# Spreading softmax reciprocals: two small transposes and eight SBUF transfers in place of four whole transposes

## The chip, the cores and the metric

The kernel runs on one core of one Trainium2 chip. The metric is the device time of one execution in microseconds (us); lower is better. A core has a tensor engine (PE, with PEld for its weight loads), a vector engine (DVE), a scalar engine (ACT), GpSimd (POOL) and a sync engine (SP), which here only issues transfers. Each works through its own instructions in order.

## The reference, cut to what matters

A decoder layer over 32 sequences of 256 tokens with 256 features: self attention with rotary positions and ALiBi, windowed cross attention, and a feed-forward block with quantized activations, each followed by a residual and a layer norm. The change is in the self attention alone:

```python
# per sequence: x [256, 256]; 16 heads of 64; 4 key/value heads
q, k = rope(x @ Wq), rope(x @ Wk)           # v = x @ Wv
attn = q @ k.T / sqrt(64) + slope[h] * (j - i)
attn = softmax(attn)                        # over the 256 keys j
out = concat_heads(attn @ v) @ Wo
x = layernorm(x + out)
```

The softmax's division by the row sums is done after the product with v: `attn @ v` is formed from the plain exponentials, and each head's output is multiplied by the reciprocal of its sums.

## The kernel before

The work of a sequence is cut into units. A self unit is 128 queries, one of two halves of the key/value heads and two of four head pairs; there are eight per sequence (`self_units`). One step of the outer loop works on the self unit of that step, and a pair of units (`m`, four per sequence) shares one set of sums, one attention output `oT` and one set of reciprocals. A step has two parts (`part` 0 and 1). The order of PE, DVE and ACT is written out by hand in this loop; the order on SP and POOL is chosen by the framework's planner.

In step 2m+2 (an even one), for pair `m`:

- `self_inverse` (L436, L438) runs first: DVE takes the reciprocal of eight columns of sums (128 queries x 8 heads) and copies it out to `wide`, 128 x 512, each column repeated 64 times.
- The generators of the other stages that are due run next: projections (L334 on PE, L343 and L350 on DVE, whose halves are exchanged by the transfers of L316), the query and key rotation of the cross attention (L553 on ACT, transfers of L558, L569 to L571 on POOL), the normed outputs, the feed-forward block (L808 to L859).
- `self_turn` transposes the exponentials `p` of the last unit on PE (L450), and ACT copies them out of PSUM (L455).
- `self_scores` makes the scores of this step's unit (L397); DVE adds the bias and finds the maximum (L413), ACT takes the exponential and sums it (L423).
- `self_values` multiplies the transposed exponentials by v (L467); ACT copies the result to `oT` (L474), where a partition is one of two heads x 64 features and a column is one of 4 x 128 queries.
- In part 1, `self_spread` (L482) transposes `wide` in four products, so that PSUM holds each reciprocal along the partitions of its head, and `self_normal` (L490) multiplies `oT` by that on DVE.

`self_output` later multiplies `oT` by Wo in two halves, in two parts of a later step (L498). Cross-attention steps (L659 scores, L673 maximum, L689 exponential, L698 transposes, L714 values, L734 and L740 back-transposes and division) run interleaved with these. `work(name, shape, bufs)` gives a buffer in SBUF, `bank(name)` one of eight in PSUM. Transfers issued as `nc.sync.dma_start` go through SP's queue.

Of the kernel before, what the change touches and what calls it, by code (L numbers as in the profile page):

```python
# [10 lines left out]
BF16 = mybir.dt.bfloat16  # L11
# [5 lines left out]
P = 128  # L17
# [8 lines left out]
H, KV, HD = 16, 4, 64  # L26
# [24 lines left out]
def kernel(  # L51
# [27 lines left out]
    nc = tc.nc  # L79
    B = x.shape[0]  # L80
# [4 lines left out]
    def ctile(shape, dtype, name):  # L85
        return const.tile(shape, dtype, name=name, tag=name)
# [3 lines left out]
    def bank(name, shape=(P, 512), dtype=F32):  # L90
        return ps.tile(list(shape), dtype, tag="b", name=name)


    ident = ctile([P, P], F32, "ident")
    make_identity(nc, ident)
    ident_b = ctile([P, P], BF16, "ident_b")
    make_identity(nc, ident_b)
    neg_half = ctile([P, 2], F32, "neg_half")
    nc.gpsimd.memset(neg_half, -0.5)

# [3 lines left out]
    def work(name, shape, bufs=2, dtype=F32):  # L104
        return sb.tile(list(shape), dtype, tag=name, name=name, bufs=bufs)

    def small(name, n):
        return sb.tile([P, 8], F32, tag="small", name=name, bufs=48)[:, 0:n]
# [87 lines left out]
    def flush():  # L196
        while last:
            last.pop(0)()
# [190 lines left out]
    def self_scores(b, i):  # L389
        s = state[b]  # L390
        qc, kc, rp = self_units[i]
        qT, kT = s["qT", 2 * kc + rp], s["kT"]
        banks = [bank("s") for _ in range(2)]
        for rr in range(2):
            for half in range(2):
                rows_ = slice(half * HD, (half + 1) * HD)
                nc.tensor.matmul(  # L397
                    banks[half][:, rr * L : (rr + 1) * L],
                    qT[rows_, rr, qc * P : (qc + 1) * P],
                    kT[rows_, kc, :],  # L400
                    start=(rr == 0),
                    stop=(rr == 1),
                )
        s["p", i] = [work("p", [P, 512], 4) for _ in range(2)]
        if rp == 0:
            s["sums", i // 2] = small("sums", 8)
        for half in range(2):
            p = s["p", i][half]
            nm = small("nm", 2)
            for rr in range(2):  # L410
                cols = slice(rr * L, (rr + 1) * L)

                nc.vector.tensor_tensor_reduce(  # L413
                    p[:, cols],
                    banks[half][:, cols],
                    alibi[:, 2 * (4 * kc + 2 * rp + rr) + half, :],
                    -0.125,
                    3.0e38,
                    ALU.add,
                    ALU.min,  # L420
                    nm[:, rr : rr + 1],
                )
                nc.scalar.activation(  # L423
                    p[:, cols],
                    p[:, cols],
                    AF.Exp,
                    bias=nm[:, rr : rr + 1],
                    scale=-1.0,
                    accum_out=s["sums", i // 2][:, (2 * rp + rr) * 2 + half : (2 * rp + rr) * 2 + half + 1],
                )  # L430

    def self_inverse(b, m):

        s = state[b]
        rinv = small("rinv", 8)
        nc.vector.reciprocal(rinv, s.pop(("sums", m)))  # L436
        s["rinv", m] = wide = work("wide", [P, 8, HD], 1)
        nc.vector.tensor_copy(wide, rinv.unsqueeze(2).to_broadcast([P, 8, HD]))  # L438

    def self_turn(b, i):  # L440
        s = state[b]
# [34 lines left out]
    def self_spread(b, m):  # L476

        s = state[b]
        wide = s.pop(("rinv", m))
        s["R", m] = pr = bank("R")  # L480
        for r in range(NCH // 2):
            nc.tensor.transpose(  # L482
                pr[:, r * P : (r + 1) * P], wide[:, 2 * r : 2 * r + 2, :].rearrange("p a e -> p (a e)"), ident
            )

    def self_normal(b, m):
        s = state[b]
        qc, kc, _rp = self_units[2 * m]
        oT = s["oT", qc, kc].rearrange("p c t -> p (c t)")
        nc.vector.tensor_tensor(oT, oT, s.pop(("R", m)), ALU.mult)  # L490
# [400 lines left out]
    with tc.manual_schedule(engines={mybir.EngineType.PE, mybir.EngineType.DVE, mybir.EngineType.Activation}):  # L891
        running = []
        slot = min(starts)
        while starts or running:
            step, part = divmod(slot, 2)
            k, odd = divmod(step - CROSS, 2)
            for gen in starts.pop(slot, ()):
                running.append([slot, gen])

            def cross(f, unit, *more):  # L900
                if 0 <= unit < 4 * B:
                    f(*divmod(unit, 4), *more)

            def own(f, unit):
                if 0 <= unit < 8 * B:
                    f(*divmod(unit, 8))


            def pair(f):
                if step % 2 == 0 and 0 <= step // 2 - 1 < 4 * B:  # L910
                    f(*divmod(step // 2 - 1, 4))

            if part == 0:
                pair(self_inverse)
            else:
                pair(self_spread)
            if part == 1 and not odd:
                cross(cross_exp, k, 0)
            if part == 0 and odd:
                cross(cross_exp, k, 1)  # L920
            for r in list(running):
                if r[0] == slot:
                    wait = next(r[1], r)
                    if wait is r:
                        running.remove(r)
                    else:
                        r[0] += wait or 1
            if part == 0:
                own(self_turn, step - 1)
                if odd:  # L930
                    cross(cross_back, k - 1)
                    cross(cross_turn, k, 0)
                else:
                    cross(cross_turn, k - 1, 1)
                while late:
                    late.pop(0)()
                flush()
                own(self_scores, step)
                if not odd:
                    cross(cross_scores, k)  # L940
                pair(self_values)
            else:
                if not odd:
                    cross(cross_values, k - 1)
                pair(self_normal)
                while late:
                    late.pop(0)()
            flush()
            slot += 1
# [89 lines left out]
```

## Time and profile before

| | |
|---|---|
| Time, median of 3 runs | 2258.0 us (2257.89 to 2258.37) |
| The profiled execution | 2257.97 us, span 2256.0 us |
| Mean granted clock of PE | 0.984 |
| PE busy | 2188.3 us, 97% of the span |
| DVE busy | 1708.6 us, 76% |
| ACT busy | 1680.8 us, 75% |
| POOL busy | 1126.7 us, 50% |
| DMA, queue 1 (SP's and the like) | 189440 packets, 136.95 MB, 24.8% of 16 engines |

The span is from the first to the last instruction of the profiled execution; its time is the device time of the same execution. Busy shares are means over all stages. PE's products are pipelined, so what a group of them costs is the distance from its start to the start of the next group. A row of a timeline has the start in us, the duration, the engine and line, the operation and the names of what is written and read; "x8" counts instructions that were merged into the row.

### The profile page before, as it was taken

The numbers are of one execution on the slowest core, as the hardware profiler recorded it, in microseconds if no ns is written. First come the engines' busy times: TensorE is split into PE (matmuls) and PEld (weight loads), VectorE is DVE, ScalarE is ACT, GpSimd is POOL, SyncE is SP. The second block draws the span as 40 slices with busy tenths as digits, with TensorE's granted clock in tenths as the row PEclk, the third lists the DMA queues.
The fourth block names the chain that finished last, engine by engine and source line by source line (L and its number), as shares of the span: only waits on it lengthen the run. The fifth ranks groups of instructions, "written<-read, shape, count | busy, mean of one in ns | idle before, by whom it ended". The sixth has DMA issues, their size and how long they took to land.

```text
span 2256.0 us, 55618 instructions
## 1 busy us (share of the span) xinstructions
PE 2188.3 (97%) x17828; PEld 1660.7 (74%) x17828; DVE 1708.6 (76%) x6949; ACT 1680.8 (75%) x4961; POOL 1126.7 (50%) x1851
## 2 busy tenths in 40 slices
PE   7999999999999999999999999999999999999983
PEld 5777777777777777777777777777777777777652
DVE  3777777877777877777877778787777887777765
ACT  2677777878777878777878777878777878777862
POOL 5345455555555555555555555555555454545432
PEclk8999999999999999999999999999999999999986
DMA  6322232222222222222222222222222222222111
GB/s 217 90 54 56 63 69 61 55 62 60 64 70 59 59 58 60 68 65 60 60 59 65 63 65 61 62 59 65 60 65 64 61 58 69 56 61 56 34 32 31
DMA packets 191426, 144.07 MB, mean 64 GB/s; under 512 B 107808, under 2 KB 160928, under 8 KB 191136
## 3 DMA queue, kind: packets, MB, share of 16 engines
q1 hardware_dynamic: 189440, 136.95, 24.8%
q8 instruction: 143, 2.34, 0.4%
q10 hardware_dynamic: 1696, 3.57, 0.4%
q14 instruction: 147, 1.20, 0.2%
HBM read 39.50 MB, written 8.39 MB: 21 GB/s over the span
## 4 chain that ended last, share of the span: by engine, by line
PE 89%; DVE 4%; ACT 3%; DMA 2%; POOL 1%; issue 1%; SPq 0%; POOLq 0%; ACTq 0%; DVEq 0%
PE proj L334 13%; PE s L397 11%; PE o L467 10%; PE wo L498 10%; PE t L450 9%; PE xt L698 5%; PE ff L808 4%; PE xs L659 3%; PE R L482 3%; PE xo L714 3%; PE xv L619 3%; PE ffo L855 2%; PE xq L535 2%; PE xw L766 2%; PE xk L607 2%; PE v L366 2%
## 5 line engine op out<-in xcount | busy, mean ns | idle before, releaser
L423 ACT ACTIVATE p<-p,nm 128x256 f32<-128x256 f32 x1024 | 508.7, 501 | 104.8 <-DVE nm L413 100.7
L413 DVE CUSTOM_DVE_ANT_0 p<-s,alibi 128x256 f32<-128x256 f32 x1024 | 372.5, 420 | 124.7 <-PE s L397 124.5
L455 ACT COPY pT<-t 128x512 f32<-128x512 f32 x512 | 273.8, 589 | 224.8 <-PE t L450 224.7
L689 ACT ACTIVATE xp<-xp,xnm 128x128 f32<-128x128 f32 x1024 | 325.8, 393 | 1.8 <-DVE xnm L673 1.8
L397 PE MATMUL s<-kT,qT 64*128 64x256 f32 x2048 | 290.4, 402 | 0.0
L450 PE MATMUL t<-ident,p 128*128 128x128 f32 x2048 | 275.2, 274 | 3.8 <-ACT p L423 2.5
L450 PEld LDWEIGHTS t<-ident,p 128*128 128x128 f32 x2048 | 238.9, 141 | 45.4 <-ACT qb L553 8.4
L467 PE MATMUL o<-pT,v 128*64 128x256 f32 x2048 | 257.0, 386 | 0.2 <-ACT pT L455 0.2
L334 PE MATMUL proj<-xT,wq_sb 128*128 128x256 f32 x1024 | 252.2, 390 | 0.0
L498 PE MATMUL wo<-wo_sb,oT 128*128 128x256 f32 x1024 | 245.3, 382 | 0.0
L358 POOL TENSOR_TENSOR qT<-qT,other 128x512 f32<-128x512 f32 x128 | 163.4, 1277 | 155.0 <-DMA other<-psin 89.8
L673 DVE CUSTOM_DVE_ANT_0 xp<-xs,mask 128x128 f32<-128x128 f32 x1024 | 225.8, 286 | 0.0
L397 PEld LDWEIGHTS s<-kT,qT 64*128 64x128 f32 x2048 | 176.2, 186 | 59.2 <-issue 41.3
L498 PEld LDWEIGHTS wo<-wo_sb,oT 128*128 128x128 f32 x1024 | 192.0, 190 | 35.5 <-issue 10.3
L467 PEld LDWEIGHTS o<-pT,v 128*64 128x64 f32 x2048 | 142.2, 136 | 99.0 <-issue 32.0
L334 PEld LDWEIGHTS proj<-xT,wq_sb 128*128 128x128 f32 x1024 | 187.8, 193 | 33.6 <-DVE xnm L673 6.0
L423 ACT ACTIVATION_READ_ACCUMULATOR p<-p,nm 128x1 f32 x1024 | 195.6, 191 | 0.0
L343 DVE TENSOR_TENSOR psin<-proj,rs_sb 128x512 f32<-128x512 f32 x160 | 110.2, 689 | 93.6 <-PE proj L334 93.3
L569 POOL TENSOR_TENSOR qb<-qb,rx_sb 128x256 f32<-128x256 f32 (+1 forms) x96 | 87.5, 911 | 184.6 <-DMA other<-qb 77.8
L700 ACT COPY xpT<-xt 128x512 f32<-128x512 f32 x256 | 153.6, 600 | 6.3 <-PE xt L698 5.5
L698 PE MATMUL xt<-ident,xp 128*128 128x128 f32 x1024 | 155.1, 274 | 0.0
L823 DVE SCALAR_TENSOR_TENSOR gu<-gu,ff 128x512 f32<-128x512 f32 x128 | 82.3, 682 | 74.6 <-ACT gu L822 74.5
(150 smaller groups left out, 4373.5 us busy)
## 6 DMA issues: line engine op xcount, KB each, us to landing
other<-psin SPq DMA_DIRECT2D x640, 64.0 KB, 2.0
xT<-in_xt_dram SPq DMA_DIRECT2D x32, 256.0 KB, 2.9
xs<-in_x_dram SPq DMA_DIRECT2D x32, 256.0 KB, 3.0
cs<-in_ctx_dram SPq DMA_DIRECT2D x32, 256.0 KB, 2.7
other<-qb SPq DMA_DIRECT2D x64, 128.0 KB, 2.0
kTz<-tr SPq DMA_DIRECT2D x256, 32.0 KB, 2.0
other<-qb SPq DMA_DIRECT2D x128, 64.0 KB, 1.9
out_dram<-x SPq DMA_DIRECT2D x32, 256.0 KB, 2.3
```

Of the source, the lines that this page charges most:

```text
L334: nc.tensor.matmul(pq[:, c * L : (c + 1) * L], w[:, dc, c * P : (c + 1) * P], xT[:, dc, :], start=(dc == 0), stop=(dc == NDC - 1),)
L358: nc.gpsimd.tensor_tensor(d2, d2, other, ALU.add)
L397: nc.tensor.matmul(banks[half][:, rr * L : (rr + 1) * L], qT[rows_, rr, qc * P : (qc + 1) * P], kT[rows_, kc, :], start=(rr == 0), stop=(r ...
L413: nc.vector.tensor_tensor_reduce(p[:, cols], banks[half][:, cols], alibi[:, 2 * (4 * kc + 2 * rp + rr) + half, :], -0.125, 3.0e38, ALU.add ...
L423: nc.scalar.activation(p[:, cols], p[:, cols], AF.Exp, bias=nm[:, rr : rr + 1], scale=-1.0, accum_out=s["sums", i // 2][:, (2 * rp + rr) * ...
L450: nc.tensor.transpose(pt[:, j * P : (j + 1) * P], p[half][:, rr * L + kk * P : rr * L + (kk + 1) * P], ident,)
L455: nc.scalar.copy(pT[half], pt)
L467: nc.tensor.matmul(po[half * HD : (half + 1) * HD, rp * L : (rp + 1) * L], s["v"][:, kk, (2 * kc + half) * HD : (2 * kc + half + 1) * HD], ...
L498: nc.tensor.matmul(py[:, 0:D], s["oT", qc, kc][:, r, :], wo_sb[:, 4 * kc + r, :], start=(kc == 0 and r == 0), stop=(kc == 1 and r == 3),)
L673: nc.vector.tensor_tensor_reduce(p[:, cols], banks[2 * half + j // 2][:, j % 2 * P : (j % 2 + 1) * P], s["mask"][:, qc, :], -1.0, 3.0e38, ...
L689: nc.scalar.activation(p[:, cols], p[:, cols], AF.Exp, bias=s["xnm", i][half][:, j : j + 1], scale=-1.0)
L698: nc.tensor.transpose(pt[:, j * P : (j + 1) * P], p[:, j * P : (j + 1) * P], ident)
```

## The change

The columns of the sums are put in another order (first the four of half 0, then the four of half 1). The reciprocals stay a 128 x 8 tile; `wide` and its copy go. `self_spread` now transposes four columns at a time, in two products that each fill 4 x 128 of a PSUM bank. DVE copies these 4 x 256 values to `rT` in SBUF. Eight transfers on SP's queue then write `R` (128 x 512 in SBUF): each reads one row of 128 values of `rT` and writes it to 64 partitions. `self_normal` multiplies `oT` by `R` from SBUF.

The calls move too: `self_spread` from part 1 to part 0 of the same step, behind `self_turn`; `self_normal` from part 1 of step 2m+2 to part 0 of step 2m+3, behind that step's `self_turn`. An identity in bf16 that nothing uses goes.

```diff
-    ident_b = ctile([P, P], BF16, "ident_b")
-    make_identity(nc, ident_b)
...
-                    accum_out=s["sums", i // 2][:, (2 * rp + rr) * 2 + half : (2 * rp + rr) * 2 + half + 1],
+                    accum_out=s["sums", i // 2][:, half * 4 + 2 * rp + rr : half * 4 + 2 * rp + rr + 1],
...
     def self_inverse(b, m):
-        rinv = small("rinv", 8)
+        s["rinv", m] = rinv = small("rinv", 8)
         nc.vector.reciprocal(rinv, s.pop(("sums", m)))
-        s["rinv", m] = wide = work("wide", [P, 8, HD], 1)
-        nc.vector.tensor_copy(wide, rinv.unsqueeze(2).to_broadcast([P, 8, HD]))
...
     def self_spread(b, m):
-        wide = s.pop(("rinv", m))
-        s["R", m] = pr = bank("R")
+        rinv = s.pop(("rinv", m))
+        pr = bank("R")
+        for half in range(2):
+            nc.tensor.transpose(pr[0:4, half * P : (half + 1) * P], rinv[:, half * 4 : half * 4 + 4], ident)
+        rT = work("rT", [4, 2 * P], 1)
+        nc.vector.tensor_copy(rT, pr[0:4, 0 : 2 * P])
+        s["R", m] = R = work("R", [P, 512], 1)
         for r in range(NCH // 2):
-            nc.tensor.transpose(
-                pr[:, r * P : (r + 1) * P], wide[:, 2 * r : 2 * r + 2, :].rearrange("p a e -> p (a e)"), ident
-            )
+            for half in range(2):
+                nc.sync.dma_start(
+                    R[half * HD : (half + 1) * HD, r * P : (r + 1) * P],
+                    rT[r : r + 1, half * P : (half + 1) * P].unsqueeze(1).to_broadcast([1, HD, P]),
+                )
...
             if part == 0:
                 pair(self_inverse)
-            else:
-                pair(self_spread)
...
             if part == 0:
                 own(self_turn, step - 1)
+                pair(self_spread)
+                if step % 2 and 0 <= step // 2 - 1 < 4 * B:
+                    self_normal(*divmod(step // 2 - 1, 4))
...
             else:
                 if not odd:
                     cross(cross_values, k - 1)
-                pair(self_normal)
```

## The prediction

> **What bounds the kernel now.** I read the page's busy shares and its chain of waits, then the groups of instructions by line, then the timelines of PE, SP, DVE and ACT around the middle of the run.
>
> The chain that ended last says where a saving counts:
>
> ```profile
> PE 89%; DVE 4%; ACT 3%; DMA 2%; POOL 1%; issue 1%; SPq 0%; POOLq 0%; ACTq 0%; DVEq 0%
> ```
>
> PE carries 89% of it, line 482 (the four transposes) about 3%. The PE timeline over one of the short stretches (start, duration, line; a group's end overlaps the next group, so what a group costs is the distance between starts):
>
> ```profile
> 1209.33 1.04 PE L450 MATMUL t<-ident,p 128*128 128x128 f32 x8
> 1210.20 0.38 PE L734 MATMUL xr<-ident,xoT 128*128 128x128 f32 x2
> ...
> 1213.90 0.66 PE L482 MATMUL R<-ident,wide 128*128 128x128 f32 x4
> 1214.39 1.03 PE L808 MATMUL ff<-ff_gate,xiT 128*128 128x512 bf16 x4
> ...
> 1223.02 1.30 PE L450 MATMUL t<-ident,p 128*128 128x128 f32 x8
> ```
>
> Eight transposes take 0.87 us (1209.33 to 1210.20), 0.109 each; the four of line 482 take 0.49, 0.05 of it the semaphore instruction that goes ahead of them in 93 of 128 cases. A sequence repeats every 67.35 us (line 334 starts at 1140.14, 1207.50, 1274.85) with hardly a gap on PE, 32 times. It holds four pairs of steps, counted from the transposes of an even step: A from 1209.33 (13.7 us), B from 1223.02 (15.45), C from 1238.47 (17.3), D from 1255.77 (20.9). Each pair makes one R and multiplies one oT.
>
> The SP queue, where the new transfers go, in pair A and into B:
>
> ```profile
> 1210.78 2.45 SPq L316 DMA_DIRECT2D other<-psin  x4
> 1219.60 5.27 SPq L643 DMA_DIRECT2D kTz<-tr  x8
> 1225.29 1.18 SPq L558 DMA_DIRECT2D other<-qb  x2
> ```
>
> One issue holds SP for 0.6 us, whatever its size (2.45 for 4, 1.18 for 2). From issue to landing:
>
> ```profile
> other<-psin SPq DMA_DIRECT2D x640, 64.0 KB, 2.0
> kTz<-tr SPq DMA_DIRECT2D x256, 32.0 KB, 2.0
> ```
>
> And what is thin on ACT at the end of pair A:
>
> ```profile
> 1219.85 0.51 ACT L423 ACTIVATE p<-p,nm 128x256 f32<-128x256 f32 x1
> ...
> 1221.84 1.27 ACT L689 ACTIVATE xp<-xp,xnm 128x128 f32<-128x128 f32 x4
> 1223.01 0.60 ACT L553 ACTIVATE qb<-xq,xbcol 128x128 f32<-128x128 f32 x2
> ```
>
> ACT runs without a break from the first self exponential to line 553, and the second half of PE's transposes at 1223.02 already waits 0.29 us for line 553 (it reads the bank that they need). So in pair A anything that delays the first line 413 on DVE delays PE by the same time. In the other pairs there is slack.
>
> [...] All eight transfers read rows 0 to 3 of rT. The trace of before has no transfer that reads one partition. [...]
>
> **The change part by part.** Removed on PE: four transposes, 0.49 us a pair. Added: two, 0.22 (0.27 with a semaphore). Gain 0.22 to 0.27 a pair, I take 0.27: 128 x 0.27 = 35 us if nothing waits. This is on the path.
>
> DVE: the copy to wide goes (128 x 0.485 = 62 us), a copy of 4 x 256 from PSUM comes (nearest rows: 0.42 for 256 columns from PSUM, 54 us at most). DVE is not the bound; nothing follows from the sum. The identity in bf16 costs POOL two instructions of 0.5 us before 1.8 us, when PE waits for weights until 4.55: nothing, and with that cover gone 0.5 us once. The column order of the sums costs nothing.
>
> New position of the transposes: right after those of p. They wait for the reciprocal. In C it ends at 1238.65 and PE gets there at 1239.34; in B at 1223.80 against 1224.19. Hidden by the eight transposes; without that cover a few tenths in a pair.
>
> The eight transfers: SP issue 8 x 0.6 = 4.9 us a pair, 128 x 4.9 = 630 us. SP has it (about 1,300 issues of 0.6 us and 128 transposing ones of 1.25 us or more, some 1,000 of 2256 us), but in order: behind them wait psin, qb and kTz transfers, and R waits behind those that come first. I take R behind the transfers whose data is ready first. The landing of the last is bounded by: below, the issue spacing, 2.0 + 7 x 0.61 = 6.3 us from the first issue; above, [...]10.3 us. I take the upper[...] and keep the lower for the range.
>
> The multiplication (0.67) moves to the next odd step, after the transposes and ahead of line 413. DVE, in order, then waits for R, and behind it stand line 413, so the exponentials, so PE's next transposes; and in B and D line 498's second half needs oT. Pair by pair, upper price:
> - A: psin's transfers hold SP until 1213.23. R has landed at 1213.23 + 10.3 = 1223.5, the multiplication ends at 1224.2, the first exponential starts 0.52 later at 1224.75 instead of 1219.85. Line 553 and PE's transposes move with it: +4.9 us.
> - B: transposes end at 1224.4 plus latency, copy until about 1225.0, R landed 1235.3, oT at 1236.0. Line 498 wants it at 1234.13, less 0.27 saved: 2.1 us of waiting, against before +2.0 with a handoff.
> - C: psin's first four hold SP until 1242.2; R landed 1252.5, exponentials from 1253.7 instead of 1252.07, line 553 done at 1257.4 where PE wants the bank at about 1256.2: +1.3, less 0.27: +1.0.
> - D: psin's until 1260.2, R landed 1270.5, line 413 stood at about 1270.1, next transposes only at 1276.68: hidden, -0.27.
>
> Sum 4.9 + 2.0 + 1.0 - 0.3 = 7.6 us per sequence, x 32 = 244: span 2256 + 244 = 2500. The profiled execution took 2257.97, 1.97 more than its span and within 0.03 of the median 2258.0; so 2502.
>
> With the lower price: A has R at 1219.5, exponentials at 1220.7, +0.9. B has R at 1232.8, before DVE comes free at 1233.8: -0.2. C -0.1, D -0.3. Sum +0.3 us, 2268. So the fate of this change hangs on pair A and on when R lands.
>
> **Rivals.** First, [...]the planner's order on SP is kind (R ahead of part of psin's transfers, or psin's ready sooner): all R are hidden, and what stays is PE's gain of 0.27 less a few tenths in A, where the multiplication now stands between line 823 and line 413: 10 to 35 us, 2223 to 2248. For it: SP is idle from 1213.2 to 1219.6 and the engines of the DMA are 25% busy. Second, the lower price as worked out above, 2255 to 2300: only A waits[...]. Third, worse than forecast: R is issued behind a waiting transfer (SP waits 281 us for psin in all, up to 7.7 at a time), or R's packets hold up the qb and psin transfers behind them and PE waits for qT or xqT: 2580 and more. The sign turns at about 0.6 us per transfer, where R in A lands before 1219. That the products do not get fewer is excluded, since two are issued for four.
>
> **How the numbers follow.** [...] 0.58, time 2502, own range 2340 (0.9 us per transfer: A +2.9, the rest about -0.5) to 2620. Lower price: 0.15. Everything hidden: 0.22. SP's order ruinous: 0.05. A measurement can tell about 0.2%, 4.5 us, from no change. Faster 0.25 (the hidden case and a little of the lower price), same 0.05, slower 0.70. The range of 2240 to 2580 leaves out about 0.1 on each side.
>
> **What would show it.** Line 482's successor: 256 products of one group of two, 0.22 us from start to start. R's transfers: 1024 of 32 KB, median landing well over 2 us (4 to 6)[...]. Idle of DVE ahead of line 490 put down to the DMA of R: some 8 us per sequence at the upper price, under 1 at the lower. PE idle for ACT at line 450 and for DVE at line 498; busy share of PE under 90%. I am wrong if DVE's idle before line 490 stays small, or if R lands in 2 us and PE waits all the same.

## The result and the profile after

The changed kernel takes 2929.67 us (2922.08 to 2940.11, 4 runs) against 2258.18 us for the kernel before, run beside it: 1.2978 times as long, 95% interval 1.2962 to 1.2993. "Slower" was forecast, but with 2502 us, and 2580 at the upper end. The loss is 671 us where 244 were forecast.

The profiled execution has a span of 2927.9 us. Lines have moved in the new file: 482 is now 478 (the products) with 484 (the transfers), 490 is 493, 316 is 314, 397 is 395, 413 is 411, 423 is 421, 436 is 434, 450 is 446, 498 is 501, 535 is 538, 553 is 556, 643 is 646, 659 is 662, 714 is 717, 808 is 811. In the experiments they shift by a few more.

The chain that ended last, by engine, on the page of the kernel after:

```profile
PE 34%; DMA 20%; SPq 19%; DVE 13%; POOL 6%; issue 5%; ACT 3%; DVEq 0%; POOLq 0%; ACTq 0%
```

PE carried 89% before. Now 39% is transfers and their issue: the kernel is no longer bound by PE, which is busy 82% of the span. The multiplication on the same page, with DVE's idle time ahead of it behind the second bar:

```profile
L493 DVE TENSOR_TENSOR oT<-oT,R 128x512 f32<-128x512 f32 x128 | 88.6, 692 | 596.7 <-DMA kTz<-tr 204.3
```

The transfers, from issue to landing (all data written) in the last column:

```profile
R<-rT SPq DMA_DIRECT2D x1024, 32.0 KB, 5.2
...
cs<-in_ctx_dram SPq DMA_DIRECT2D x32, 256.0 KB, 6.2
...
kTz<-tr SPq DMA_DIRECT2D x256, 32.0 KB, 2.3
```

and one line of the page before:

```profile
cs<-in_ctx_dram SPq DMA_DIRECT2D x32, 256.0 KB, 2.7
```

R's 32 KB take 5.2 us to land, kTz's 32 KB take 2.3. Others land later too: the load of cs went from 2.7 us to 6.2.

Pair A in the SP timeline of the kernel after (the prediction shows the same stretch without R):

```profile
1404.21 2.49 SPq L804 DMA_TRANSPOSE xiT<-xib  x2
1406.80 0.53 SPq L110 DMA_DIRECT2D xT<-in_xt_dram  x1
1407.43 2.47 SPq L314 DMA_DIRECT2D other<-psin  x4
1410.00 6.50 SPq L484 DMA_DIRECT2D R<-rT  x8
1416.61 6.66 SPq L646 DMA_DIRECT2D kTz<-tr  x8
```

Eight issues of R hold SP for 6.50 us: the first five take up to 0.60 us each, the last three 0.87, 1.15 and 1.26. That the queue pushes back on the issuer is a reading of this; no run isolates it. In the trace these eight transfers land from 1413.22 to 1421.56: the first 3.2 us after its issue, the others one after another, 1.19 us apart in the mean. And the same pair on DVE, on ACT and on PE:

```profile
1421.94 0.69 DVE L493 TENSOR_TENSOR oT<-oT,R 128x512 f32<-128x512 f32 x1 [6.47 <-DMA kTz<-tr]
1422.55 0.42 DVE L411 CUSTOM_DVE_ANT_0 p<-s,alibi 128x256 f32<-128x256 f32 x1
```

```profile
1423.07 0.51 ACT L421 ACTIVATE p<-p,nm 128x256 f32<-128x256 f32 x1 [6.69 <-DVE nm L411]
```

```profile
1403.95 1.04 PE L446 MATMUL t<-ident,p 128*128 128x128 f32 x8
...
1416.05 1.04 PE L811 MATMUL ff<-ff_up,xiT 128*128 128x512 bf16 x4
1423.38 2.08 PE L538 MATMUL xq<-zT,xq_w 128*128 128x128 f32 x8 [6.29 <-DVE nm L411]
...
1426.82 1.89 PE L811 MATMUL ff<-ff_up,xiT 128*128 128x512 bf16 x4
1428.50 1.26 PE L446 MATMUL t<-ident,p 128*128 128x128 f32 x8
```

DVE stands idle 6.47 us ahead of the multiplication. The bracket names a kTz transfer, but line 493 reads nothing of kTz: it waits for R's eight transfers, the last of which, issued at 1415.24, lands at 1421.56. The name is only that of a transfer in the queue near it. Behind the multiplication stands line 411.

PE then stops for 6.29 us at line 538, put down to line 411. No input of line 538 comes from line 411; what they share is a PSUM bank. `bank` hands out eight in turn: counted from the scores ahead of the stop, two go to these scores, four to the cross scores (line 662) and two to the feed-forward products (line 811), so line 538 gets the first bank of the scores again, and may write there only when line 411 has read it. The times agree: the second of the two instructions of line 411 that read this bank ends at 1423.31, and PE goes on at 1423.38.

When PE goes on, the same work takes longer: line 811 took 1.04 us at 1416 and takes 1.89 at 1426. The share of the clock granted to PE shows why. The trace has it in pieces of 3.41 us; here the pieces around this stop, and two around a shorter one in pair C (stretch, its length, PE busy with its instructions, granted clock, DMA share, GB/s):

```profile
1415.31:1418.72 3.41, 1.78 (x18) 1.00 0.71 26
1418.72:1422.13 3.41, 0.00 (x0) 1.00 0.64 61
1422.13:1425.54 3.41, 2.16 (x10) 0.50 0.18 41
1425.54:1428.96 3.42, 3.42 (x41) 0.50 0.11 38
1428.96:1432.37 3.41, 3.41 (x31) 1.00 0.12 7
...
1463.10:1466.51 3.41, 1.36 (x22) 1.00 0.30 83
1466.51:1469.92 3.41, 3.41 (x9) 0.50 0.01 5
```

After the stop PE runs at half its clock, until 1428.96. In pair C the half clock, 0.50 from 1466.51, follows a stop of only 2.00 us:

```profile
1465.62 0.64 PE L717 MATMUL xo<-xpT,xvaug 128*32 128x128 f32 x16 [2.00 <-DVE nm L411]
1466.31 3.62 PE L332 MATMUL proj<-xT,wq_sb 128*128 128x256 f32 x8
```

The same eight products of line 332 took 1.99 us at 1402.12.

### The profile page after: what moved, and what is told of

Same layout as the page of the kernel before. It is cut to its first block, busy times and chain, and to the rows that moved or that the text cites. A ratio compares the mean times of both kernels' runs of the same rounds, so it can differ in the third digit from the quotient of the medians.

```text
span 2927.9 us, 56259 instructions
## 1 busy us (share of the span) xinstructions
PE 2392.1 (82%) x17572; PEld 1744.4 (60%) x17572; DVE 1703.7 (58%) x6949; ACT 1694.8 (58%) x4961; POOL 1108.4 (38%) x1849
## 4 chain that ended last, share of the span: by engine, by line
PE 34%; DMA 20%; SPq 19%; DVE 13%; POOL 6%; issue 5%; ACT 3%; DVEq 0%; POOLq 0%; ACTq 0%
SPq L484 13%; DMA R<-rT 7%; PE proj L332 6%; DMA other<-psin 6%; PE wo L501 5%; DVE p L411 4%; DMA kTz<-tr 3%; SPq L314 3%; PE o L463 3%; DVE oT L493 3%; PE t L446 2%; PE s L395 2%; PE xo L717 2%; PE xq L538 2%; SPq L646 2%
## 5 line engine op out<-in xcount | busy, mean ns | idle before, releaser
L493 DVE TENSOR_TENSOR oT<-oT,R 128x512 f32<-128x512 f32 x128 | 88.6, 692 | 596.7 <-DMA kTz<-tr 204.3
L501 PE MATMUL wo<-wo_sb,oT 128*128 128x256 f32 x1024 | 303.5, 449 | 153.7 <-DVE oT L493 153.6
L501 PEld LDWEIGHTS wo<-wo_sb,oT 128*128 128x128 f32 x1024 | 223.6, 225 | 213.7 <-DVE oT L493 177.4
L446 PE MATMUL t<-ident,p 128*128 128x128 f32 x2048 | 282.1, 281 | 16.6 <-ACT p L421 16.3
L446 PEld LDWEIGHTS t<-ident,p 128*128 128x128 f32 x2048 | 250.5, 146 | 61.7 <-ACT p L421 24.0
L332 PE MATMUL proj<-xT,wq_sb 128*128 128x256 f32 x1024 | 266.7, 407 | 1.3
L538 PE MATMUL xq<-zT,xq_w 128*128 128x128 f32 x512 | 101.1, 358 | 185.4 <-DVE nm L411 185.4
L332 PEld LDWEIGHTS proj<-xT,wq_sb 128*128 128x128 f32 x1024 | 196.3, 201 | 40.4 <-DVE nm L411 8.8
L538 PEld LDWEIGHTS xq<-zT,xq_w 128*128 128x128 f32 x512 | 85.9, 254 | 210.9 <-DVE nm L411 200.2
L600 POOL TENSOR_SCALAR mask<-ck,cq_sb 64x128 f32<-64x128 f32 (+1 forms) x96 | 70.6, 736 | 311.8 <-DVE xnm L676 305.8
```

The costliest lines, as they stand in the source:

```text
L332: nc.tensor.matmul(pq[:, c * L : (c + 1) * L], w[:, dc, c * P : (c + 1) * P], xT[:, dc, :], start=(dc == 0), stop=(dc == NDC - 1),)
L446: nc.tensor.transpose(pt[:, j * P : (j + 1) * P], p[half][:, rr * L + kk * P : rr * L + (kk + 1) * P], ident,)
L501: nc.tensor.matmul(py[:, 0:D], s["oT", qc, kc][:, r, :], wo_sb[:, 4 * kc + r, :], start=(kc == 0 and r == 0), stop=(kc == 1 and r == 3),)
L538: nc.tensor.matmul(pq[:, ch * P : (ch + 1) * P], xq_w[:, dc, ch * P : (ch + 1) * P], zqT[:, dc, :], start=(dc == 0), stop=(dc == NDC - 1),)
```

## The experiments

All times are medians, each beside the kernel before, run with it (2256.9 to 2258.7 us). In the cuts, `...` stands for lines left out. The first set asked what makes R late. Theory 1 in the expectations is that reading from the same few partitions, here 0 to 3, sets the pace: in the kernel after R's transfers land 1.24 us apart in the median.

**Rows four partitions apart.** As after, with the eight rows in partitions 0, 4, ... 28:

```diff
-        nc.vector.reciprocal(rinv, s.pop(("sums", m)))
+        r8 = small("rinv", 8)
+        nc.vector.reciprocal(r8, s.pop(("sums", m)))
+        s["rinv", m] = rinv = work("rinv32", [P, 32], 2)
+        nc.vector.tensor_copy(rinv.rearrange("p (a e) -> p a e", e=4), r8.unsqueeze(2).to_broadcast([P, 8, 4]))
...
-            nc.tensor.transpose(pr[0:4, half * P : (half + 1) * P], rinv[:, half * 4 : half * 4 + 4], ident)
...
+        nc.tensor.transpose(pr[0:32, 0:P], rinv, ident)
...
-                    rT[r : r + 1, half * P : (half + 1) * P].unsqueeze(1).to_broadcast([1, HD, P]),
+                    rT[4 * (4 * half + r) : 4 * (4 * half + r) + 1, :].unsqueeze(1).to_broadcast([1, HD, P]),
```

> The eight reciprocal rows are copied out [...](rows 0, 4, ... 28; one product of 32 columns in place of two of four, and one more small copy on DVE). Everything else as after. Theory 1 ([...]1.2 us or more each, so R lands late): median landing of R falls from 5.2 us to 2.0-2.6, issues take 0.6 us again, the time falls to 2240-2330. Theory 2 (the price is that of eight issues and eight landings on SP's queue, whatever they read): landing stays at 4-5 us, the time stays above 2800.

2401.29 us, ratio 1.063 (1.0611 to 1.0648). The landing fell to 2.8 us, a little over what theory 1 said; the time did not fall as far as it said. So moving the rows apart takes away 528 of the 671 us, and 143 have another cause.

**Rows in partitions 0 to 7.** One product of the eight columns as they are:

```diff
-            nc.tensor.transpose(pr[0:4, half * P : (half + 1) * P], rinv[:, half * 4 : half * 4 + 4], ident)
...
+        nc.tensor.transpose(pr[0:8, 0:P], rinv, ident)
...
-                    rT[r : r + 1, half * P : (half + 1) * P].unsqueeze(1).to_broadcast([1, HD, P]),
+                    rT[1 * (4 * half + r) : 1 * (4 * half + r) + 1, :].unsqueeze(1).to_broadcast([1, HD, P]),
```

> As after, but one product of all eight columns, so the eight rows lie in partitions 0 to 7[...]. Theory 1: [...]landing about 2.7-3.5 us, time 2350-2650[...]. Theory 2: landing 4-5 us, above 2800.

2403.63 us, ratio 1.0637 (1.0621 to 1.0653), landing 2.8 us: no different from rows four partitions apart. In both, R's transfers land 0.63 to 0.64 us apart (median), close to the 0.61 us that one issue holds SP; in the kernel after they land 1.24 us apart. Rows in partitions 0 to 7 are spread enough, and what is left is the spacing of the issues.

**Rows 32 or 64 partitions on.** To tell whether it is how many partitions are read that counts, or which, two kernels that differ in one number, the partition at which half 1's rows begin (`off` is 32 or 64; the columns in between hold ones):

```diff
+        nc.tensor.transpose(pr[0 : 2 * off, 0:P], rinv_wide, ident)
...
+                    rT[half * off + r : half * off + r + 1, :].unsqueeze(1).to_broadcast([1, HD, P]),
```

> The rows of half 0 lie in partitions 0 to 3 and those of half 1 in partitions 32 to 35: eight partitions, each read by one transfer[...]. One product of 64 columns makes them; the rest as after. [...]as after, 2850-2950 us, median landing about 5 us. Rival (what hurts after is that a partition is read by two transfers, or that they are few partitions): as with rows 0 to 7, 2390-2420, landing 2.8 us.

> The same kernel as the run before it, with half 1 in partitions 64 to 67 in place of 32 to 35[...]. [...]2385-2420 us, landing 2.8 us. Rival: no difference to the run before it.

2924.7 us with 32 (ratio 1.2957, 1.2938 to 1.2976) and 2401.39 us with 64 (1.0638, 1.0622 to 1.0654). From the lists of transfers, first with 32, then with 64:

```profile
R<-rT SPq DMA_DIRECT2D x1024, 32.0 KB, 5.2
```

```profile
R<-rT SPq DMA_DIRECT2D x1024, 32.0 KB, 2.8
```

Eight partitions, each read once, are as slow as four read twice when the second half begins at partition 32, and 523 us faster when it begins at 64. So it is neither the number of partitions nor that each is read twice: what counts in these runs is which partitions the rows lie in.

**No transfers.** The products and places of after, with a constant in place of R, so that the division is left out:

```diff
-        s["R", m] = R = work("R", [P, 512], 1)
-        for r in range(NCH // 2):
...
+        s["R", m] = R_const
```

> As after, with the eight transfers left out: line 493 multiplies by a constant tile of ones in place of R (so the division by the sums is left out). Shows what the rest of the change is worth. Theory 1 and 2 both: 2223-2250, the gain of two products a pair with everything hidden. Theory 3 (the new places of the products and of the multiplication make PE wait by themselves): above 2300.

2277.51 us, ratio 1.0084 (1.0069 to 1.0099). Neither expectation held: without a single transfer the change still costs 19 us. Who PE waited for most in this kernel (total us, times, longest):

```profile
PE wo L497 <- DVE oT L489: 19.4, 30, 1.6
```

Line 497 is the output product. In B it comes to DVE's multiplication before DVE has got there.

**The old place.** The same, with the multiplication back in part 1 of the even step:

```diff
-                if step % 2 and 0 <= step // 2 - 1 < 4 * B:
-                    self_normal(*divmod(step // 2 - 1, 4))
...
                     cross(cross_values, k - 1)
+                pair(self_normal)
```

> As the run without transfers (line 493's multiplier is a constant, the division by the sums is left out), with the multiplication back in part 1 of the even step, where it stood before. Separates the new place from the two products less. If the place is what cost the run without transfers its gain: 2220-2235. If the two products less are worth nothing: 2255-2280.

2250.86 us, ratio 0.997 (0.996 to 0.998): faster than before, by 7 us and not by the 28 to 35 that the products alone were to be worth. So the new place of the multiplication costs about 27 us, and three quarters or more of the products' gain is missing. Part of what is missing is shown by PE's waits in this kernel:

```profile
PE R L480 <- DVE rinv L436: 10.8, 21, 1.8
```

The products now stand where the reciprocal is sometimes not ready; in the old place, some four microseconds later, PE never waited for it. Where the rest went was not traced.

**Load without waiting.** All transfers as in after, but the multiplication reads a constant table (the division is left out here too):

```diff
-        nc.vector.tensor_tensor(oT, oT, s.pop(("R", m)), ALU.mult)
+        s.pop(("R", m))
+        nc.vector.tensor_tensor(oT, oT, rx_sb[:, 0, :, :].rearrange("p a t -> p (a t)"), ALU.mult)
```

> As after, with all transfers issued and landing in R, but line 493 multiplies by a constant table, so nobody waits for them (the division by the sums is left out). Separates the load on SP and on the DMA engines from the wait on DVE. Theory 1 with the wait as the main cost: 2230-2330. If the load itself holds up the transfers of psin, qb and kTz behind it, so that PE waits for qT and xqT: above 2600.

2498.83 us, ratio 1.1059 (1.1041 to 1.1078): between the two expectations. 221 us more than without transfers, though nothing multiplies by R. (The next copy into `rT` still has to wait until the transfers have read it; ahead of that copy DVE stands idle for only 6 us in all.) Part of the cost is seen in the waits of POOL, DVE and PE in this kernel:

```profile
POOL qT L356 <- DMA other<-psin: 266.6, 63, 11.3
```

```profile
DVE row L523 <- POOL rs_x L519: 131.4, 60, 9.1
```

```profile
PE R L478 <- DVE rinv L434: 60.2, 28, 3.3
```

POOL works in order and waits for the late transfers of psin; the small steps of a layer norm stand behind that on POOL, DVE waits for them, and PE for DVE's reciprocal. PE's 60 us are a part of the 221; the rest was not traced.

**The same load from partitions 0 to 7.** The edits of the rows in partitions 0 to 7 and of the constant table together.

> As after with the rows in partitions 0 to 7 ([...]one product), all transfers issued, but nobody waits for them (a constant multiplies, the division by the sums is left out). If the load of 2499 us[...]: 2265-2310. If it came from 1024 more issues on SP's queue: above 2400.

2281.6 us, ratio 1.0111 (1.0093 to 1.0128): 4 us more than without transfers. POOL's wait for psin is 121 us here where it was 267, and DVE's wait for POOL

```profile
DVE row L522 <- POOL rs_x L518: 22.4, 45, 4.0
```

1024 more issues on SP's queue, all 34 MB and 81920 more packets cost nearly nothing, 4 us; it was having all eight read from partitions 0 to 3 that held up the others.

**A and C later.** With rows in partitions 0 to 7, the multiplication of A and C one step later:

```diff
+                if step % 2 == 0 and 0 <= step // 2 - 2 < 4 * B and step // 2 % 2 == 0:
+                    self_normal(*divmod(step // 2 - 2, 4))
                 pair(self_spread)
-                if step % 2 and 0 <= step // 2 - 1 < 4 * B:
+                if step % 2 and 0 <= step // 2 - 1 < 4 * B and (step // 2 - 1) % 2:
                     self_normal(*divmod(step // 2 - 1, 4))
```

> Rows in partitions 0 to 7, and the multiplication of pairs A and C (whose oT is wanted two steps later) moved one more step back, ahead of the next pair's copy of its rows; B and D as after. Theory (the wait ahead of the maximum in pair A, with PE stopped by the PSUM bank that the maximum reads): PE's wait at the query projection of the cross attention, 60 us in the run with rows in 0 to 7, goes; 2300-2345 against 2404. If that wait is not on the path: 2380-2410.

2327.3 us, ratio 1.03 (1.0275 to 1.0326). As expected: 76 us gone, and PE's wait for a bank at the query projection (60 us with rows in 0 to 7) no longer among its waits. Left is

```profile
PE wo L500 <- DVE oT L492: 77.1, 32, 3.6
```

once per sequence, in B. It was 41 us with rows in 0 to 7.

**The output product later.** The edit before, and `at(s0 + 2 * (5 + 4 * t) + 1, self_output(b, t))`.

> As the run before it, and the output product of the self attention starts one slot later, so that its second half comes a part after the multiplication of B and D. If the remaining cost is PE's wait of 41 us at that product: 2235-2290, perhaps under before. If moving it makes later stages late: above 2320.

2400.22 us, ratio 1.0632 (1.0613 to 1.065): a miss. The wait at the output product went, and two others came, at the transposes of the normed row and at the projections, where the name of line 411 again points to a bank:

```profile
PE zqT L206 <- DVE row L521: 66.6, 33, 2.1
PE proj L332 <- DVE nm L411: 60.6, 29, 2.6
```

Everything that follows the output product moved a slot with it.

**Two queues.** Half 1's four transfers issued from POOL, then from ACT (`(nc.sync, nc.gpsimd)[half].dma_start`, `(nc.sync, nc.scalar)[half].dma_start`), on the version with A and C later.

> The version with rows in partitions 0 to 7 and A and C later (2327 us), with the four transfers of half 1 issued from POOL's queue. If what is left is the time that SP needs to issue eight in B: PE's wait of 77 us at line 500 falls under 40 and the time to 2270-2300. If POOL's issues cost its other work more: above 2330.

> As the run before it, with half 1 issued from ACT's queue. The same gain in landing for B, against four issues of 0.6 us a pair in ACT's order, which wait for the copy of the rows: 2270-2320 if ACT has the room, above 2330 if its exponentials come late.

2422.95 us (ratio 1.0713, 1.0674 to 1.0752) and 2633.8 us (1.1678, 1.1635 to 1.1721) against 2327: both worse. From POOL, landing became 4.8 and 5.3 us (POOL's and SP's) and the wait at line 500 stayed at 76 us; why landing got slower was not tried. From ACT, ACT's own order was blocked: copies that stand behind the issues waited 183 us that the trace puts down to transfers of R.

No version tried that computes the reference's division beats the kernel before.

## Why the prediction was right or wrong

**Right: the direction, the late landing and the wait ahead of the maximum.** This is the case that the forecast gave 0.58. Read from partitions 0 to 3, R lands late, after 5.2 us in the median against 2.8 from partitions 0 to 7; DVE waits in order ahead of the maximum; PE waits behind that. The runs with 32 and 64, 5.2 and 2.8 us, show that it depends on which partitions are read. The upper bound for the last landing, 10.3 us, was my estimate, which no trace of before showed. In A the landings are 1.19 us apart in the trace after, and seven of these on top of the 2.0 us make the same 10.3: one transfer short, since the first of the eight also needs its turn and came after 3.2. With eight the sum is 11.5 us; 11.55 were measured. Of the signs named, R's landing (5.2 us, forecast 4 to 6) and PE's busy share (82%, forecast under 90%) came. DVE's idle time ahead of the multiplication came larger: 597 us, 18.6 per sequence, where 8 were forecast.

**Right: the size of the products.** Two products take 0.22 us a pair, as estimated: with four stationary columns (line 478) each takes the same 0.109 us from start to start as with 128 (line 446). Less came of it than their length, as the old place shows.

**Wrong: what a late R costs PE.** From one start of line 446 to the next, in the sequence shown, and in the last column the difference of the means over all such pairs of the run:

| Pair | before | after | difference | forecast | over the run |
|---|---|---|---|---|---|
| A | 13.7 | 24.55 | +10.9 | +4.9 | +10.8 |
| B | 15.45 | 20.4 | +5.0 | +2.0 | +6.0 |
| C | 17.3 | 20.8 | +3.5 | +1.0 | +2.6 |
| D | 20.9 | 20.55 | -0.35 | -0.27 | +1.3 |

A sequence is about 21 us longer in the mean (671 / 32), and 7.6 were forecast. D agrees in this sequence by luck of the choice: over the run PE waited 24 times in D at the output product, 24.6 us together, so R was not hidden there either.

The failed step is the sum for A, and in it the sentence that anything that delays the first line 413 "delays PE by the same time": R comes later than the sum has it, and PE loses more than the delay. In A the forecast is 6 us short, and three terms make this up.

First, R started later: T + 6.05 and not T + 3.90 (T is the start of the transposes), 2.15 us. I put only psin's transfers ahead of R on SP. The transposing transfers of xiT and the load of xT go ahead of psin's. Before, they held SP from T - 1.77 to T + 1.3; after the change DVE makes xib 1.6 us later, and they hold it from T + 0.26 to T + 3.4. Second, the landing took 1.2 us longer, for the eighth transfer, and the multiplication began 0.4 us after it. So the exponentials start 19.1 us after the transposes and not 15.4.

Third, the clock, 2.4 us. PE does not run on to its next transposes and wait there, as the sum has it. It stops at line 538, for a PSUM bank, and has the query projection, the values and half of the feed-forward block still to do. At full clock that would have cost A little: these products took 2.7 us before (1220.35 to 1223.02), and with 2.7 PE would have come to its transposes within 0.2 us of where the forecast chain behind the exponentials puts them. They took 5.1. The sum had no term for the clock. In B and C the products behind the stop took 1.4 and 1.6 us longer than before, in C behind a piece of 3.41 us in which PE was busy for 1.36.

Over the run PE waited most in this kernel

```profile
PE xq L538 <- DVE nm L411: 185.4, 30, 7.4
PE wo L501 <- DVE oT L493: 153.6, 56, 5.8
PE xo L717 <- DVE nm L411: 83.2, 32, 7.5
```

422 us together; the forecast had such waits at line 498 (now 501) alone, and placed the others at the transposes, where PE waits 16 us in all. I took slack at the next transposes for slack everywhere. PE was busy 2392.1 us, and in the kernel without transfers, with the same 17572 products, 2181.7: 210 us. The two, 422 less the 19 that the kernel without transfers waits, and 210, make 613 of the 652 us between those two kernels. Of the 210 the half clock explains about 179: PE was busy for 405 us at half clock after the change and for 47 in the kernel without transfers, and half of that time is the excess.

**Wrong: the load was to be hidden.** The third rival had the queue behind R hurting, at 0.05. With the rows in partitions 0 to 3 the load alone, nothing multiplying by R, costs 221 us; with rows in 0 to 7 it costs 4. So the issues on SP, which I counted with care, were not the price, and reading all eight from partitions 0 to 3, which I counted only for R's own landing, was.

**Wrong: the rival of everything hidden.** At best it was to be 2223 to 2248. With no transfers at all it is 2277.5, and with the multiplication in its old place 2250.9. The new place costs about 27 us, where I allowed "a few tenths in A": DVE reaches the multiplication in B only after a reduction chain of the feed-forward block, and PE needs oT at once. The products' saving was also not worth its own length: earlier in the step they meet a reciprocal that is not ready.

Multiplications beside a large instruction on POOL took longer; no run isolates why. With rows in partitions 0 to 7, 29 multiplications that began beside a 128x1024 instruction on POOL took 1.54 us in the mean, the 65 that began beside an idle POOL 0.69, and 28 beside a 128x1 instruction also 0.69. In the kernel after, POOL was idle at the start of all 128, which took 0.69. It is off the main account.

## What to carry to other kernels

When a wait is put ahead of an engine's in-order work, follow it to the first instruction of the critical engine that needs anything from behind it, buffers and PSUM banks included; that is where it stops, and the work after it is added, at the clock that a trace shows behind such a stop (here line 811 took 1.89 us behind it, at 0.50, and 1.04 ahead of it). Count a transfer's load on the partitions it reads as well as on its queue, and try other partitions for the sources: with half 1's rows from partition 32 on R landed in 5.2 us and cs in 6.3, with them from 64 on in 2.8 and 3.1. A shorter piece of work on the bound engine is worth its length only if its inputs are ready at the place where it is put. And read a forecast's pairs off several sequences: one that agrees may be the exception.

## What the runs showed of the hardware that was not expected

- Partitions 0 to 3 as the source of eight transfers of 32 KB: median landing 5.2 us, the landings 1.24 us apart, against 2.8 us and 0.63 to 0.64 apart with the rows in partitions 0 to 7 or four apart. Issue of such a transfer held SP for 0.77 us in the mean, against 0.61.
- Transfers that read none of these rows land late too: cs from HBM 6.2 us against 2.7, 6.3 when nothing multiplies by R.
- Issuing half the transfers from POOL made all of R's slower to land, 4.8 and 5.3 us against 2.8.
- In the trace of the kernel after, the clock granted to PE changes only at the bounds of pieces of 3.41 us, and what it is in one goes with how busy PE was in the piece before. From 60 us after the start to 120 before the end, all 72 full-clock pieces in which PE was busy under 45% were followed by one at half clock, and none of the 578 in which it was busy over 57%. From half clock it came back after each of the 75 pieces in which PE was busy over 82.5%, and after none of the 64 below.
